# Three attention layers and a gate on one core: block sums in a scratch tile, a clip moved behind the exponential, biases added at the transposes

## The chip, the cores and the metric

The kernel runs on one core of a Trainium2 chip. The core has TensorE (matrix products into the eight banks of PSUM), VectorE, ScalarE and GpSimd for work on elements, and queues that start DMAs. The engines run side by side, each through its own instructions in order, and wait for each other at semaphores. The metric is the device time of one execution in microseconds (us), the median of several; the profile comes from one further execution with its own time.

## The reference

Sixteen samples of 256 channels by 32 x 32 positions (1024 tokens) pass through four layers. All numbers are float32.

```python
# layer 0: attention over tokens, on a group norm with 8 groups
xn = group_norm(x, gamma, beta)
q, k, v = split(einsum('bchw,oc->bohw', xn, w_qkv) + b_qkv)
out = softmax(q^T k / sqrt(256)) v ;  x = einsum(w_proj, out) + b_proj + x
# layer 1: a gate for each position
weight1, weight2 = mean(x, over channels), max(x, over channels)
weight3 = relu(conv3x3([weight1, weight2], w1, b1))
x = x * sigmoid(conv3x3(weight1 + weight2 + weight3, w2, b2))
# layer 2: as layer 0, with separate wq, wk, wv, wp and their biases
# layer 3: queries and keys of 32 channels, clipped logits
energy = clip(einsum('bqn,bqm->bnm', q, k) * 32**-0.5, -10, 10)
out = gamma * (v softmax(energy)^T) + x
```

In all three attentions the rows of the softmax add up to one, so a constant added to every value comes out of the attention as that same constant.

## The kernel before

**Folding.** At the start `fold` (L213) multiplies the weights of layers 0 and 2 together: `m` is the product of the query and key weights, `wvp` that of the value and output weights, and `brow` is the row of all value and output biases, on every partition. Layer 3 keeps its own weights `w3`, and `vg3` is its value bias times gamma.

**Two streams.** `sample(b)` (L683) is a generator that emits the work of one sample in small steps and yields after each. Two such streams, one over the even and one over the odd samples, are advanced in turn (L800 to L810); the first is ahead by `OFFSET` = 26 steps. A framework then assigns the semaphores and settles each engine's order, so that between two steps of one stream usually lies one of the other. While a sample is in layer 3, `head` (L672) loads sample b + 2, transposes it (`to_tokens`, L296) and normalizes it (`group_norm`, L87).

**PSUM.** All products use one pool of eight banks of 128 x 512 (`bank`, L183). A bank is used again when the last reader of its earlier content is done.

**One attention** (`attend`, L632; for layer 3 `clipped_attend`, L730) has these stages:

- `t = m x` in four products (L642) and, for the blocked products that follow, sums and differences `xs` of blocks of x (L656 to L659);
- the values (`values`, L326): four banks `vps`, each moved to `vt` with the bias added by VectorE (L663, or L752 in layer 3, which multiplies by gamma as well); then four combinations of value blocks (`tv`, L353 to L357). GpSimd writes columns of ones next to the values (L331, L351), so that the products also give the sums of the softmax;
- for each half of 512 queries, the logits. Layers 0 and 2 use seven block products in place of eight (`logits`, L387), whose sums are put together in the tile `e` by ScalarE copies (L435, L437, L444, L452) and VectorE additions (L432), and take the exponential on ScalarE (L448, L455). Layer 3 packs four 32-row products into four banks (L763), VectorE clips each bank into `e` (L772), and ScalarE takes the exponential of two at a time (L775);
- `weighted` (L458): the product of `e` with the values, again seven block products in place of eight. VectorE forms four combinations of `e` (L469, L470, L502, L505). Seven groups of eight products (each product is two instructions) go to three banks. Bank b holds the first product, then has `s2 t2` and later `s3 t3` added to it on TensorE, and is read in between; bank af holds two single products; bank c holds `s1 t1` and then has `s4` added. Each read is an `add` (L491): on VectorE, y = bank * ri + y, where `ri` is the reciprocal of the row sum (L510, L515) and y is the residual. A group that adds to a bank may start only when the reads of its earlier content are done.

After layer 0 comes the gate: VectorE takes sum and maximum over channels (L698), two small convolutions as products with banded matrices (`gate_of`, L124) give `sg`, VectorE multiplies the eight token blocks by it (L708), and TensorE transposes back to channels (`to_channels`, L317, with a ScalarE copy out of PSUM). `group_norm` computes statistics on VectorE (L93, L94), averages them over groups with two tiny products (`gm` L98, `gv` L107), a power on GpSimd (L111), and scales both blocks of channels on VectorE (L118). After layer 2 and layer 3 the tokens are transposed to channels in the same way; layer 3 sends them out by SyncE's queue (L781).

`count`, `alike` and `moderate` check that the sums and weights are in a safe range; otherwise a general path runs afterwards (`general_path`), which does not happen with these inputs.

Of the kernel before, what the change touches and what calls it, by code (L numbers as in the profile page):

```python
# [26 lines left out]
EPS = 1e-5  # L27

# [58 lines left out]
def group_norm(nc, k, small, psum, ptag, xt, out, gamma, beta, nm):  # L87
# [29 lines left out]
    for c in range(CC):  # L117
        nc.vector.tensor_scalar(  # L118
            out[:, c, :], xt[:, c, :], a[:, c : c + 1], bb[:, c : c + 1], ALU.mult, ALU.add
        )  # L120
# [40 lines left out]
def fast_path(nc, tc, k, bad, x, w_l0, w_l2, w_l3, qk_bias, v_bias, out):  # L161
# [7 lines left out]
    with ExitStack() as ctx:  # L169
# [30 lines left out]
        vcol = wts.tile([P, 2, CC], FP, name="vcol")  # L200
        for i in range(2):
            nc.sync.dma_start(vcol[:, i, :], v_bias[i].rearrange("(c p) -> p c", p=P))
        w3 = wts.tile([P, CC, 2 * DQK + C], FP, name="w3")
        nc.scalar.dma_start(w3, w_l3.rearrange("(c p) o -> p c o", p=P))
        vb3 = wts.tile([P, C], FP, name="vb3")
        nc.scalar.dma_start(vb3, v_bias[2:3, :].to_broadcast([P, C]))
# [6 lines left out]
        def fold(nm, which, base):  # L213
# [42 lines left out]
            nc.vector.tensor_scalar(tb, ps[:, :CC], C**-0.5, None, ALU.mult)  # L256

# [22 lines left out]
        vg3 = wts.tile([P, C], FP, name="vg3")  # L280
        gam = k.sc[:, S_GAMMA : S_GAMMA + 1]

        def fold3():
            for g in range(G4):
                i = g // 2
                nc.gpsimd.tensor_copy(
                    w3r[:, :, g * DQK : (g + 1) * DQK], w3[:, :, i * DQK : (i + 1) * DQK]
                )
            nc.vector.tensor_scalar(qb[:PH], qb[:PH], DQK**-0.5, None, ALU.mult)
            nc.vector.tensor_scalar(vg3, vb3, gam, None, ALU.mult)  # L290
# [5 lines left out]
        def to_tokens(xt, nm):  # L296

            xr = tokp.tile([P, NT, C], FP, tag="tok", name=f"xr_{nm}")
            for t2 in range(NT // 2):
# [17 lines left out]
        def to_channels(y, dst, h, c, nm):  # L317
# [6 lines left out]
            nc.scalar.copy(dst, ps)  # L324
# [133 lines left out]
        def weighted(e, vt, tv, y, ri, h, nm):  # L458
# [32 lines left out]
            def add(t, cs, ps):  # L491
                r = ri[:, t : t + 1]
                nc.vector.scalar_tensor_tensor(  # L493
                    y[:, t, cs], ps, r, y[:, t, cs], ALU.mult, ALU.add
                )
# [10 lines left out]
            go(a(1, 1), t4, af[:, 1])  # L506
            yield
# [41 lines left out]
        def alike(w, bias, nm):  # L549
# [14 lines left out]
            nc.vector.tensor_tensor(size[:, C:], bias, bias, ALU.mult)  # L564
            nc.vector.tensor_tensor(size[:, :C], ps[:, :C], size[:, C:], ALU.add)
# [59 lines left out]
        def checks():  # L625
# [4 lines left out]
            alike(w3[:, :, 2 * DQK :], vb3, "l3")  # L630

        def attend(xt, y, weights, nm):  # L632
# [27 lines left out]
            rows = brow.rearrange("p (o j c) -> p o j c", o=1, j=CC).to_broadcast([P, 2, CC, P])  # L660
# [22 lines left out]
        def sample(b):  # L683
# [6 lines left out]
            yield from attend(xt, xr, folded["l0"], f"l0_{b}")  # L690
# [15 lines left out]
            for h in range(NH):  # L706
                for t in range(h * TPH, (h + 1) * TPH):
                    nc.vector.tensor_scalar(  # L708
                        xr[:, t, :], xr[:, t, :], sg[:, t : t + 1], None, ALU.mult
                    )  # L710
                for c in range(CC):
                    to_channels(xr, x1[:, c, h * HALF : (h + 1) * HALF], h, c, f"x1_{b}")
# [17 lines left out]
        def clipped_attend(xt, y, b):  # L730

# [387 lines left out]
```

## Time and profile before

| | us |
|---|---|
| median of 3 runs | 3098.36 |
| all three | 3100.22, 3097.28, 3098.36 |
| the profiled execution | 3098.49 |
| its span, first to last instruction | 3096.6 |

The mean granted clock of TensorE was 0.986 of full speed. The kernel moves 19.56 MB in and 16.78 MB out, 12 GB/s over the span, so memory traffic is no subject here. The page gives, for each engine, the busy time; for groups of instructions (line, engine, operation, output <- input, shape) the busy time, the mean duration of one and the idle time of the engine just before them with what ended it. Groups that matter below (columns as described):

```profile
L493 DVE SCALAR_TENSOR_TENSOR xr_l<-b_l,ri_l,xr_l 128x128 f32<-128x128 f32 x256 | 77.9, 346 | 23.3 <-PE b_l L367 21.0
...
L532 DVE SCALAR_TENSOR_TENSOR xr_l<-b_l,ri_l,xr_l 128x256 f32<-128x256 f32 x128 | 56.1, 480 | 65.4 <-PE b_l L367 65.1
```

In these rows DVE is VectorE, ACT ScalarE, POOL GpSimd, PE TensorE and PEld its loading of weights. A matmul instruction of the list is half of one float32 product, so the counts are twice those of the code. A wait for several semaphores is put down to the one that came last.

### The profile page before, as it was taken

What the parts mean: (1) busy time and instruction counts of PE and PEld (TensorE: products, weight loads), DVE (VectorE), ACT (ScalarE), POOL (GpSimd) and SP (SyncE); (2) the same over time, 40 slices, a digit from 0 to 9 for tenths busy, and PEclk for the clock granted to TensorE, in tenths of its full rate; (3) what the DMA queues carried; (4) which work ended last, traced back from release to release, by engine and by line L of the source; (5) the groups of instructions that cost most, each with busy time, mean ns of one, the idle gap of its engine ahead of it and who ended that gap; (6) DMA issues with size and microseconds to landing.
All of it is one profiled execution on the core that took longest, in us unless ns stands there. A gap on an engine that the chain in (4) does not pass through costs nothing.

```text
span 3096.6 us, 44611 instructions
## 1 busy us (share of the span) xinstructions
PE 2937.3 (95%) x18586; PEld 2528.2 (82%) x18586; DVE 2203.7 (71%) x4587; ACT 933.6 (30%) x1329; POOL 55.6 (2%) x231
## 2 busy tenths in 40 slices
PE   7999999999999999999999999999999999999997
PEld 6878878878888788788887887888878888788886
DVE  8677776777766767677676777677776677767675
ACT  1223233233233332333232322323333323223232
POOL 0000000000000000000000000000000000000000
PEclk9999999999999999999999999999999999999999
DMA  1000000000000000000000000000000000000000
GB/s 64 1 1 14 21 14 8 1 14 28 8 8 1 14 28 8 8 1 14 28 15 1 15 1 28 15 1 14 1 28 15 1 15 20 9 15 1 1 8 22
DMA packets 16159, 39.25 MB, mean 13 GB/s; under 512 B 2640, under 2 KB 3152, under 8 KB 15952
## 3 DMA queue, kind: packets, MB, share of 16 engines
q1 hardware_dynamic: 14560, 33.56, 3.1%
q8 instruction: 148, 2.42, 0.3%
q10 hardware_dynamic: 1392, 2.78, 0.2%
q14 instruction: 59, 0.48, 0.1%
HBM read 19.56 MB, written 16.78 MB: 12 GB/s over the span
## 4 chain that ended last, share of the span: by engine, by line
PE 79%; DVE 18%; ACT 1%; issue 1%; POOL 1%; DMA 1%; ACTq 0%; DVEq 0%
PE b_l L367 13%; PE vps_l L337 10%; PE sb_l L367 10%; PE c_l L367 10%; PE tp_l L642 7%; PE sc_l L367 7%; PE af_l L367 6%; PE sa_l L367 4%; PE sf_l L367 4%; DVE e L772 3%; PE qk L739 2%; DVE cb_l L469 2%; PE s L763 2%; DVE xr_l L493 2%; PE yp_x L321 1%; DVE e_l L432 1%
## 5 line engine op out<-in xcount | busy, mean ns | idle before, releaser
L367 PEld LDWEIGHTS b_l<-vt_l,e_l 128*128 128x128 f32 x2048 | 245.3, 192 | 21.1 <-DVE xr_l L493 7.9
L367 PE MATMUL b_l<-vt_l,e_l 128*128 128x128 f32 x2048 | 255.9, 276 | 6.1 <-DVE xr_l L493 5.6
L337 PE MATMUL vps_l<-wvp_l,x 128*128 128x256 f32 x1024 | 242.7, 380 | 0.0
L642 PE MATMUL tp_l<-x,m_l 128*128 128x512 f32 x512 | 230.2, 592 | 0.0
L435 ACT COPY e_l<-sb_l 128x512 f32<-128x512 f32 x128 | 75.2, 588 | 464.0 <-PE sb_l L367 464.0
L775 ACT ACTIVATE e<-e 128x1024 f32<-128x1024 f32 x128 | 134.3, 1055 | 258.1 <-DVE e L772 251.1
L337 PEld LDWEIGHTS vps_l<-wvp_l,x 128*128 128x128 f32 x1024 | 189.9, 190 | 23.7 <-DVE tap L82 0.2
L444 ACT COPY e_l<-sb_l 128x512 f32<-128x512 f32 x128 | 75.0, 586 | 426.0 <-PE sb_l L367 424.9
L367 PE MATMUL c_l<-tv_l,cb_l 128*128 128x129 f32 x1536 | 192.9, 277 | 0.0
L367 PEld LDWEIGHTS c_l<-tv_l,cb_l 128*128 128x128 f32 x1536 | 183.8, 192 | 6.7 <-issue 5.3
L367 PE MATMUL c_l<-vt_l,e_l 128*128 128x129 f32 x1024 | 135.7, 288 | 43.1 <-DVE xr_l L493 42.2
L448 ACT ACTIVATE e_l<-e_l 128x1024 f32<-128x1024 f32 x128 | 135.4, 1057 | 129.0 <-DVE e_l L432 128.1
L642 PEld LDWEIGHTS tp_l<-x,m_l 128*128 128x128 f32 x512 | 94.1, 190 | 94.8 <-issue 84.6
L367 PEld LDWEIGHTS c_l<-vt_l,e_l 128*128 128x128 f32 x1024 | 126.9, 200 | 53.7 <-issue 43.5
L432 DVE TENSOR_TENSOR e_l<-sc_l,e_l 128x512 f32<-128x512 f32 x128 | 88.3, 690 | 111.0 <-PE sc_l L367 111.0
L650 ACT ACTIVATE t_l<-tp_l,tb_l 128x512 f32<-128x512 f32 x128 | 88.0, 687 | 251.5 <-PE tp_l L642 251.2
L772 DVE TENSOR_SCALAR e<-s 128x512 f32<-128x512 f32 x256 | 159.6, 685 | 5.6 <-PE s L763 5.6
L455 ACT ACTIVATE e_l<-e_l 128x1024 f32<-128x1024 f32 x128 | 135.1, 1061 | 55.6 <-DVE e_l L432 54.1
L367 PE MATMUL sa_l<-t_l,x 128*128 128x256 f32 x512 | 139.7, 397 | 0.0
L367 PEld LDWEIGHTS b_l<-vt_l,e 128*128 128x128 f32 x1024 | 123.8, 194 | 16.9 <-ACT e L775 8.0
L367 PE MATMUL sf_l<-tc_l,x 128*128 128x256 f32 x512 | 137.6, 393 | 0.0
L367 PE MATMUL sb_l<-tc_l,xs_l 128*128 128x256 f32 x512 | 134.2, 382 | 1.3 <-ACT e_l L435 1.3
(190 smaller groups left out, 5931.4 us busy)
## 6 DMA issues: line engine op xcount, KB each, us to landing
x<-in_x_dram SPq DMA_DIRECT2D x32, 512.0 KB, 4.4
out_dram<-oc SPq DMA_DIRECT2D x64, 256.0 KB, 2.2
raw_l<-in_w_l_dram ACTq DMA_DIRECT2D x2, 1024.0 KB, 7.8
w<-in_w_l_dram ACTq DMA_DIRECT2D x1, 320.0 KB, 4.0
tidx<-in_tap_idx_dram ACTq DMA_DIRECT2D x1, 192.0 KB, 6.6
vb<-in_v_bias_dram ACTq DMA_DIRECT2D x1, 128.0 KB, 6.4
qb<-in_qk_bias_dram SPq DMA_DIRECT2D x4, 0.1 KB, 5.8
vcol<-in_v_bias_dram SPq DMA_DIRECT2D x2, 1.0 KB, 7.3
```

What stands on the lines that cost most here:

```text
L337: nc.tensor.matmul(ps[:, i * C : (i + 1) * C], src[:, c, t * P : (t + 1) * P], w[:, c, col : col + C], start=(c == 0), stop=(c == CC - 1),)
L367: mm = nc.tensor.matmul(out, left, right, start=fresh and m == 0 and (lone or i == 0), stop=(m == len(pairs) - 1), skip_group_check=True,)
L432: nc.vector.tensor_tensor(dst, two(ps), dst, ALU.add)
L435: nc.scalar.copy(block(0, 0), two(b))
L444: nc.scalar.copy(block(0, 1), two(b))
L448: nc.scalar.activation(e[:, m : m + 2, :], e[:, m : m + 2, :], AF.Exp)
L455: nc.scalar.activation(e[:, m : m + 2, :], e[:, m : m + 2, :], AF.Exp)
L469: nc.vector.tensor_tensor(s1, a(1, 0), a(1, 1), ALU.add)
L642: nc.tensor.matmul(ps, m[:, c, o * P : (o + 1) * P], xt[:, c, hs], start=(c == 0), stop=(c == CC - 1),)
L650: nc.scalar.activation(tt[:, o, hs], ps, AF.Identity, bias=tb[:, o : o + 1], scale=C**-0.5)
L772: nc.vector.tensor_scalar(e[:, mm, :], ss[g], -10.0, 10.0, ALU.max, ALU.min)
L775: nc.scalar.activation(part, part, AF.Exp)
```

## The change

The change has these parts:

- **Block sums.** `weighted` gets a scratch tile `acc`. ScalarE copies the first content of each block (`acc[lo, c1]`, `acc[hi, c2]`, `acc[lo, c2]`, `acc[hi, c1]`), VectorE adds the others to it (`plus`, 256 elements each), and when a token block is complete, `done` computes y = acc * ri + y once for 256 channels. `s2 t2` is now emitted ahead of `s4`.
- **Layer 3 clip.** ScalarE takes the exponential straight from the PSUM bank, and GpSimd clips two at a time to exp(-10) and exp(10).
- **Value biases.** Layers 2 and 3 no longer add the bias to the values; ScalarE copies these out (layer 3 with gamma as scale). The bias of layer 2 is added at the transposes of its result (`bcol2`), and that of layer 3 at the output's transposes, together with `bcol2` (the tokens y do not hold it) as `bcol3`. A third bias column is loaded in place of the row `vb3`.
- **Gate.** A function `planes`, called after each half of layer 0, takes the maximum on VectorE and the mean on ScalarE (a copy with an accumulated sum, one for each token block). ScalarE multiplies every other token block by the gate.
- **Norm and tokens.** `group_norm` scales its second block of channels on ScalarE; `to_tokens` copies all four banks by ScalarE and yields twice in place of three times.

```diff
+EXP_MIN, EXP_MAX = math.exp(-10.0), math.exp(10.0)
...
-    for c in range(CC):
-        nc.vector.tensor_scalar(
-            out[:, c, :], xt[:, c, :], a[:, c : c + 1], bb[:, c : c + 1], ALU.mult, ALU.add
-        )
+    nc.vector.tensor_scalar(out[:, 0, :], xt[:, 0, :], a[:, 0:1], bb[:, 0:1], ALU.mult, ALU.add)
+    nc.scalar.activation(
+        out[:, 1, :], xt[:, 1, :], AF.Identity, bias=bb[:, 1:2], scale=a[:, 1:2]
+    )
...
-        vcol = wts.tile([P, 2, CC], FP, name="vcol")
-        for i in range(2):
+        vcol = wts.tile([P, 3, CC], FP, name="vcol")
+        for i in range(3):
             nc.sync.dma_start(vcol[:, i, :], v_bias[i].rearrange("(c p) -> p c", p=P))
         w3 = wts.tile([P, CC, 2 * DQK + C], FP, name="w3")
         nc.scalar.dma_start(w3, w_l3.rearrange("(c p) o -> p c o", p=P))
-        vb3 = wts.tile([P, C], FP, name="vb3")
-        nc.scalar.dma_start(vb3, v_bias[2:3, :].to_broadcast([P, C]))
+
+        bcol2 = wts.tile([P, CC], FP, name="bcol2")
+        bcol3 = wts.tile([P, CC], FP, name="bcol3")
...
+            if nm == "l2":
+
+                ps = bank(f"brp_{nm}")
+                for c in range(CC):
+                    for o in range(CC):
+                        nc.tensor.matmul(
+                            ps[:, c : c + 1],
+                            wp[:, o, c * P : (c + 1) * P],
+                            vcol[:, which, o : o + 1],
+                            start=(o == 0),
+                            stop=(o == CC - 1),
+                        )
+                nc.vector.tensor_tensor(bcol2, ps[:, :CC], k.vec[:, :, base + 4], ALU.add)
+                return m, wvp, tb, None
...
-            nc.vector.tensor_scalar(vg3, vb3, gam, None, ALU.mult)
+            nc.vector.scalar_tensor_tensor(
+                bcol3, vcol[:, 2, :], gam, bcol2, ALU.mult, ALU.add
+            )
...
+                nc.scalar.copy(dst, ps)
                 if t2 % 2:
-                    nc.vector.tensor_copy(dst, ps)
-                else:
-                    nc.scalar.copy(dst, ps)
                     yield xr
-            yield xr
...
-            nc.scalar.copy(dst, ps)
+            if bias is None:
+                nc.scalar.copy(dst, ps)
+            else:
+                nc.scalar.activation(dst, ps, AF.Identity, bias=bias[:, c : c + 1])
...
-            def add(t, cs, ps):
-                r = ri[:, t : t + 1]
+            c1, c2 = slice(0, P), slice(P, C)
+            lo, hi = slice(0, 2), slice(2, 4)
+            acc = combp.tile([P, TPH, C], FP, tag="acc", name=f"acc_{nm}_{h}")
+
+            def plus(ts, cs, ps):
+                nc.vector.tensor_tensor(acc[:, ts, cs], ps, acc[:, ts, cs], ALU.add)
+
+            def done(i):
+                t = h * TPH + i
                 nc.vector.scalar_tensor_tensor(
-                    y[:, t, cs], ps, r, y[:, t, cs], ALU.mult, ALU.add
-                )
-
-            c1, c2 = slice(0, P), slice(P, C)
+                    y[:, t, :], acc[:, i, :], ri[:, t : t + 1], y[:, t, :], ALU.mult, ALU.add
+                )
+
             b = bank(f"b_{nm}_{h}")[:, : 2 * P].rearrange("p (i c) -> p i c", i=2)
             go(a(0, 0), vb(0, 0), b, lone=False)
+            nc.scalar.copy(acc[:, lo, c1], b)
             yield
             af = bank(f"af_{nm}_{h}").rearrange("p (w i c) -> p w i c", w=2, i=2)
             nc.vector.tensor_tensor(s2, s1, s2, ALU.subtract)
...
             yield
             nc.vector.tensor_tensor(s4, s4, s2, ALU.subtract)
             go(a(1, 1), t4, af[:, 1])
+            plus(lo, c1, af[:, 0])
             yield
             c = bank(f"c_{nm}_{h}")[:, : 2 * (P + 1)].rearrange("p (i c) -> p i c", i=2)
             go(s1, t1, c, lone=False)
             nc.vector.reciprocal(ri[:, n1 : n1 + 2], c[:, :, P])
-            for i in range(2):
-                add(n1 + i, c2, c[:, i, :P])
+            nc.scalar.copy(acc[:, hi, c2], c[:, :, :P])
+            yield
+            go(s2, t2, b, fresh=False)
+            nc.scalar.copy(acc[:, lo, c2], b)
             yield
             go(s4, vb(1, 1, P + 1), c, fresh=False)
             nc.vector.reciprocal(ri[:, n0 : n0 + 2], c[:, :, P])
+            plus(lo, c2, c[:, :, :P])
             for i in range(2):
-                add(n0 + i, c1, b[:, i, :])
-            for i in range(2):
-                add(n0 + i, c2, c[:, i, :P])
-            for i in range(2):
-                add(n0 + i, c1, af[:, 0, i, :])
-            yield
-            go(s2, t2, b, fresh=False)
-            for i in range(2):
-                add(n0 + i, c2, b[:, i, :])
+                done(i)
             yield
             go(s3, t3, b, fresh=False)
-            for i in range(2):
-                add(n1 + i, c1, af[:, 1, i, :])
-            for i in range(2):
-                t = n1 + i
-                nc.vector.scalar_tensor_tensor(
-                    y[:, t, :].rearrange("p (j c) -> p j c", j=CC),
-                    b[:, i : i + 1, :].to_broadcast([P, CC, P]),
-                    ri[:, t : t + 1],
-                    y[:, t, :].rearrange("p (j c) -> p j c", j=CC),
-                    ALU.mult,
-                    ALU.add,
-                )
+            nc.scalar.copy(acc[:, hi, c1], b)
+            plus(hi, c2, b)
+            plus(hi, c1, af[:, 1])
+            for i in range(2, 4):
+                done(i)
             yield
 
...
-                    nc.vector.tensor_tensor(dst, ps, rows, ALU.add)
+                    if brow is None:
+                        nc.scalar.copy(dst, ps)
+                    else:
+                        nc.vector.tensor_tensor(dst, ps, rows, ALU.add)
...
+                if then is not None:
+                    then(h)
...
+            def planes(h):
+                ts = slice(h * TPH, (h + 1) * TPH)
+                nc.vector.tensor_reduce(
+                    pl[:, 1, 1 + h * TPH : 1 + (h + 1) * TPH], xr[:, ts, :], AX.X, ALU.max
+                )
+                for t in range(h * TPH, (h + 1) * TPH):
+                    junk = work.tile([P, HALF], FP, tag="oc", name=f"junk_{b}_{t}", bufs=3)
+                    nc.scalar.activation(
+                        junk[:, :C],
+                        xr[:, t, :],
+                        AF.Copy,
+                        scale=1.0 / C,
+                        accum_out=pl[:, 0, 1 + t : 2 + t],
+                    )
+
+            yield from attend(xt, xr, folded["l0"], f"l0_{b}", planes)
             if b == 0:
                 k.build_toep(nc, work)
             elif b == 1:
                 checks()
-            for h in range(NH):
-                ts = slice(h * TPH, (h + 1) * TPH)
-                for i, op in enumerate((ALU.add, ALU.max)):
-                    nc.vector.tensor_reduce(
-                        pl[:, i, 1 + h * TPH : 1 + (h + 1) * TPH], xr[:, ts, :], AX.X, op
-                    )
-            nc.vector.tensor_scalar(pl[:, 0, :], pl[:, 0, :], 1.0 / C, None, ALU.mult)
...
-                    nc.vector.tensor_scalar(
-                        xr[:, t, :], xr[:, t, :], sg[:, t : t + 1], None, ALU.mult
-                    )
-                for c in range(CC):
-                    to_channels(xr, x1[:, c, h * HALF : (h + 1) * HALF], h, c, f"x1_{b}")
+                    if t % 2:
+                        nc.scalar.activation(
+                            xr[:, t, :], xr[:, t, :], AF.Copy, scale=sg[:, t : t + 1]
+                        )
+                    else:
+                        nc.vector.tensor_scalar(
+                            xr[:, t, :], xr[:, t, :], sg[:, t : t + 1], None, ALU.mult
+                        )
+                for c in range(CC):
+                    to_channels(xr, x1[:, c, h * HALF : (h + 1) * HALF], h, c, None, f"x1_{b}")
...
-                for c in range(CC):
-                    to_channels(xr, x2[:, c, h * HALF : (h + 1) * HALF], h, c, f"x2_{b}")
+                hs = slice(h * HALF, (h + 1) * HALF)
+                for c in range(CC):
+                    to_channels(xr, x2[:, c, hs], h, c, bcol2, f"x2_{b}")
...
-                    nc.vector.scalar_tensor_tensor(dst, ps, gam, rows, ALU.mult, ALU.add)
+                    nc.scalar.activation(dst, ps, AF.Copy, scale=gam)
...
-                        nc.vector.tensor_scalar(e[:, mm, :], ss[g], -10.0, 10.0, ALU.max, ALU.min)
+                        nc.scalar.activation(e[:, mm, :], ss[g], AF.Exp)
                         if g % 2:
                             part = e[:, mm - 1 : mm + 1, :]
-                            nc.scalar.activation(part, part, AF.Exp)
+                            nc.gpsimd.tensor_scalar(
+                                part, part, EXP_MIN, EXP_MAX, ALU.max, ALU.min
+                            )
...
-                    to_channels(y, oc, h, c, f"o_{b}")
+                    to_channels(y, oc, h, c, bcol3, f"o_{b}")
```

More of the change, by code (lines that the diff above doesn't have):

```diff
@@ L1 @@
+import math
 from contextlib import ExitStack
@@ L279, in fast_path @@
         w3r = wts.tile([P, CC, P], FP, name="w3r")
-        vg3 = wts.tile([P, C], FP, name="vg3")
         gam = k.sc[:, S_GAMMA : S_GAMMA + 1]
@@ L309, in to_tokens, with to_channels @@
                 dst = xr[:, 2 * t2 : 2 * t2 + 2, :].rearrange("p t c -> p (t c)")
+                nc.scalar.copy(dst, ps)
                 if t2 % 2:
-                    nc.vector.tensor_copy(dst, ps)
-                else:
-                    nc.scalar.copy(dst, ps)
                     yield xr
-            yield xr
-        def to_channels(y, dst, h, c, nm):
+        def to_channels(y, dst, h, c, bias, nm):
             ps = bank(f"yp_{nm}_{h}_{c}")
@@ L563, in alike @@
             size = work.tile([P, HALF], FP, tag="oc", name=f"sz_{nm}", bufs=3)
-            nc.vector.tensor_tensor(size[:, C:], bias, bias, ALU.mult)
-            nc.vector.tensor_tensor(size[:, :C], ps[:, :C], size[:, C:], ALU.add)
+            if bias is None:
+                nc.vector.tensor_copy(size[:, :C], ps[:, :C])
+            else:
+                nc.vector.tensor_tensor(size[:, C:], bias, bias, ALU.mult)
+                nc.vector.tensor_tensor(size[:, :C], ps[:, :C], size[:, C:], ALU.add)
             ends = small.tile([P, 2], FP, tag="ends", name=f"ends_{nm}")
@@ L629, in checks, with attend @@
                 moderate(m, tb, base, nm)
-            alike(w3[:, :, 2 * DQK :], vb3, "l3")
-        def attend(xt, y, weights, nm):
+            alike(w3[:, :, 2 * DQK :], None, "l3")
+        def attend(xt, y, weights, nm, then=None):
             m, wvp, tb, brow = weights
@@ L659, in attend @@
             nc.vector.tensor_tensor(xs[:, 3], xt[:, 1, lo], xs[:, 1], ALU.subtract)
-            rows = brow.rearrange("p (o j c) -> p o j c", o=1, j=CC).to_broadcast([P, 2, CC, P])
+            if brow is not None:
+                rows = brow.rearrange("p (o j c) -> p o j c", o=1, j=CC)
+                rows = rows.to_broadcast([P, 2, CC, P])
             for vt, dst, ps, tv in values(xt, wvp, 0, nm):
                 if tv is None:
-                    nc.vector.tensor_tensor(dst, ps, rows, ALU.add)
+                    if brow is None:
+                        nc.scalar.copy(dst, ps)
+                    else:
+                        nc.vector.tensor_tensor(dst, ps, rows, ALU.add)
                 yield
@@ L689, in sample @@
             nc.gpsimd.memset(gp, 0.0)
-            yield from attend(xt, xr, folded["l0"], f"l0_{b}")
+            def planes(h):
[13 more added lines that the diff above has]
+            yield from attend(xt, xr, folded["l0"], f"l0_{b}", planes)
             if b == 0:
@@ L707, in sample @@
                 for t in range(h * TPH, (h + 1) * TPH):
-                    nc.vector.tensor_scalar(
-                        xr[:, t, :], xr[:, t, :], sg[:, t : t + 1], None, ALU.mult
-                    )
+                    if t % 2:
+                        nc.scalar.activation(
+                            xr[:, t, :], xr[:, t, :], AF.Copy, scale=sg[:, t : t + 1]
+                        )
+                    else:
+                        nc.vector.tensor_scalar(
+                            xr[:, t, :], xr[:, t, :], sg[:, t : t + 1], None, ALU.mult
+                        )
                 for c in range(CC):
-                    to_channels(xr, x1[:, c, h * HALF : (h + 1) * HALF], h, c, f"x1_{b}")
+                    to_channels(xr, x1[:, c, h * HALF : (h + 1) * HALF], h, c, None, f"x1_{b}")
                 yield
@@ L748, in clipped_attend @@
                 yield
-            rows = vg3.rearrange("p (o j c) -> p o j c", o=1, j=CC).to_broadcast([P, 2, CC, P])
             for vt, dst, ps, tv in values(xt, w3, 2 * DQK, f"l3_{b}"):
                 if tv is None:
-                    nc.vector.scalar_tensor_tensor(dst, ps, gam, rows, ALU.mult, ALU.add)
+                    nc.scalar.activation(dst, ps, AF.Copy, scale=gam)
                 yield
```

## The prediction

> **What bounds the kernel now.** I read the page's busy shares first, then the groups by shape, then what TensorE waited for, then the time line of one period.
>
> ```profile
> PE 2937.3 (95%) x18586; PEld 2528.2 (82%) x18586; DVE 2203.7 (71%) x4587; ACT 933.6 (30%) x1329; POOL 55.6 (2%) x231
> ...
> PE 79%; DVE 18%; ACT 1%; issue 1%; POOL 1%; DMA 1%; ACTq 0%; DVEq 0%
> ```
>
> The chain that ended last is TensorE for 79% and VectorE for 18%; ScalarE and GpSimd hardly appear in it and are mostly idle. So TensorE's own work is the floor, and VectorE is what keeps TensorE off it. The first question is how far off.
>
> ```profile
> 767.00:1146.00 379.00, 363.42 (x2310) 313.09 (x2310) 270.12 (x556) 116.64 (x167) 6.65 (x26) 0.99 0.04 12
> ```
>
> The stretches table (columns: stretch, length, busy of PE, PEld, DVE, ACT, POOL, granted clock) repeats itself: two samples take 378.9 us, eight times. In undisturbed stretches the time line gives 1.785 us for 16 products of 128 columns (111.6 ns each), 1.73 us for 8 of 256 (216 ns), 3.44 us for 8 of 512 (430 ns), 1.07 us for 8 of the packed 32-row form (134 ns) and 0.876 us for 8 transposes (109.5 ns). Per period there are 1344, 640, 80, 64 and 128 of these: 150.0 + 138.4 + 34.4 + 8.6 + 14.0, plus some 5 for the small ones = 350.5 us. So 378.9 - 350.5 = 28.4 us of each period (227 us over eight) is waiting; 15.6 of the 28.4 stand as idle, the rest lies inside groups drawn longer than their cadence. What ends the idle part:
>
> ```profile
> PE c_l L367 <- DVE xr_l L493: 44.1, 33, 2.8
> PE gv_l L107 <- DVE d_l L104: 21.1, 10, 10.0
> PE gm_l L98 <- DVE mv_l L94: 18.5, 9, 2.2
> PE s L763 <- DVE e L772: 14.8, 7, 2.1
> PE yp_x L321 <- DVE xr_l L708: 12.6, 8, 1.6
> PE b_l L367 <- DVE xr_l L493: 10.2, 18, 0.9
> PE af_l L367 <- ACT e L775: 9.2, 9, 1.1
> ```
>
> (Columns: total us, times, longest.) Nearly all are VectorE, late by its queue: `c_l` waits because the second group into bank c may only start when the reciprocal and two adds have read the first, and they stand behind other work. The time line of the worst case:
>
> ```profile
> 1073.08 0.16 DVE L510 RECIPROCAL ri_l<-c_l 128x2 f32<-128x2 f32 x1
> ...
> 1073.88 1.53 DVE L118 TENSOR_SCALAR x<-x,a_l,bb_l 128x1024 f32<-128x1024 f32 x2
> 1075.32 0.60 DVE L493 SCALAR_TENSOR_TENSOR xr_l<-c_l,ri_l,xr_l 128x128 f32<-128x128 f32 x2
> 1075.84 2.48 DVE L772 TENSOR_SCALAR e<-s 128x512 f32<-128x512 f32 x4
> 1076.07 3.04 PE L367 MATMUL c_l<-vt_l,e_l 128*128 128x129 f32 x16 [2.76 <-DVE xr_l L493]
> 1077.22 2.19 ACT L775 ACTIVATE e<-e 128x1024 f32<-128x1024 f32 x2 [16.37 <-DVE e L772]
> ```
>
> The reader sees the other stream's norm and clip queue around the adds, TensorE waiting 2.76 us, and ScalarE free for 16.37 us.
>
> **The change, engine by engine.** VectorE loses: the clip L772, 159.6 us; L752, 47.9; L663 for layer 2, half of 88.1 = 44; the sum half of L698 and L701, 41; half of L118, 24.5; half of L708, 18; L311, 22. The block adds were 77.9 + 77.4 + 77.3 + 39.0 + 38.6 + 37.0 + 56.1 + 28.0 = 431 us; they become, 96 times, 4 `plus` of 256 elements (0.42 us, as L400's row) and 4 `done` (0.48, as L532's) = 347. In all 357 + 84 = 441 less: 1763 us, 58%.
>
> ScalarE gains, with copies at 588 ns per 512 (L435), so some 375 per 256: 384 first sums, 144 us; layer 2 and 3 values, 64 x 0.59 + 64 x 0.69 = 82; exponentials straight from PSUM, 256 x 0.66 (between L435 and L650) less 134.3 = 35; half norms, 32 x 1.1 (L448) = 35; 32 token copies 19, 64 gate products 28, 128 channel sums at about 0.45 = 58, bias on 128 transposes 13. Together 414: 1348 us, 44%. Neither is a bound by its sum.
>
> GpSimd gains 128 clips of 128x1024, an operation the trace does not have. Its memsets (204 ns for 128 elements, 104 for 4) give 0.8 ns per element and 0.95 us, the lower end; its copy of 64 in 235 ns, over a memset's 100 ns of start, gives 2.1 and 2.26 us, the upper; the affine select, 128 in 292 ns, is the nearest (one input from SBUF, computed): 1.5 ns and 1.6 us, which I take. The Trainium skill (GPSIMD Engine Reference, Engine selection) calls one-input operations roughly line-rate; at its 1.2 GHz that would be an estimate of 0.85 us plus a start, and the sum below would lose its 12 us of clip cost.
>
> What changes on the path, over the run:
>
> 1. `c_l` and `b_l` behind L493, 54.3 us idle. The first sums are copied by ScalarE, and `s2 t2` now lies between the two groups into bank c, while `s4` lies between the last two into bank b: a full group of 1.79 us and a step of the other stream more. The reciprocals stay on VectorE and still read bank c first. I take 45 gained.
> 2. Stretch of those groups: `c_l<-vt_l,e_l` is busy 135.7 us where 1024 x 111.6 ns is 114. Half, 10.
> 3. Layer 3 logits: 14.8 idle, and the 512 products are busy 108.2 where 134 ns each makes 68.6, 39.6 more. Eight evictions take ScalarE 8 x 0.66 = 5.3 us against VectorE's 4.9, but ScalarE's queue is empty there, where L772 started at 796.68 for products done from 791.9. In its place come the other stream's copies and exponentials, 4.5 us per four steps. Half of 54.4, 27.
> 4. `yp_x` behind L708: half of the products go to ScalarE, 6 of 12.6.
> 5. `gm` and `gv`: their short chain stays on VectorE, with less queued before it: 8 of 39.6.
> 6. `planes` writes into the three buffers that the output tiles use, so a ScalarE copy could wait for an output's landing (2.2 us, at most 32 x 2.2 = 70). In the period the outputs start near 828, 863, 1110 and 1144 us, and the halves of layer 0 end near 850, 901, 936 and 985: 13 us apart or more, so 0.
> 7. Start: the layer 2 bias row and one 128 KB load go, small transfers and products come; under 1 us beside work that bounds, taken as 0.
>
> Gains 96. Costs: after the last exponential the old order had nothing more to do, now two clips. From the first logits product, the fourth clip ends at 1.4 + 4 x 1.6 = 7.8 us against 4.9 + 1.06 = 6.0 before; TensorE comes to the first product that reads it (`af`) after 1.07 + 1.73 + 1.07 + 1.73 + 1.79 + 1.73 = 9.1 us. So the other stream's steps hide it while a clip stays under (9.1 - 1.4) / 4 = 1.9 us; without that cover, as in the last sample, each half is 1.8 us late. Behind the clips stand `rstd` and the ones columns on GpSimd, and behind `s1 = a + b` on VectorE, which waits for the last clip, the other stream's adds. I charge 12 for this, and 4 for ScalarE copies met late. At the end of each half, copy, two adds and two `done` take about 1.9 us where 0.88 stood; a step of the other stream (1.7 us or more) covers it, and without it 96 x 1.0 us would be lost at most.
>
> Net 96 - 16 = 80. The profiled run took 3098.49 (span 3096.6 and 1.9 around it), 0.1 over the median of 3098.36: **3018 us**.
>
> A sign against the clip shows already: `rstd`, 694 ns as a median, took 1.13 when VectorE read two SBUF tensors.
>
> ```profile
> 790.14 0.69 DVE L354 TENSOR_TENSOR tv_l<-vt_l,tv_l 128x512 f32<-128x512 f32 x1
> 790.25 1.13 POOL L111 TENSOR_TENSOR rstd_l<-ve_l,neg_half 128x2 f32<-128x2 f32 x1 [26.86 <-DVE ve_l L109]
> ...
> 923.24 0.69 POOL L111 TENSOR_TENSOR rstd_l<-ve_l,neg_half 128x2 f32<-128x2 f32 x1 [14.56 <-DVE ve_l L109]
> ```
>
> VectorE's operations with two SBUF inputs (block combinations 470, tv 132, xs 87, tc 108, and now `done`, which had PSUM before, 184) fill about a third of the time; a clip would lose a third of 0.5 us, 0.17, and end under the 1.9 still. The Trainium skill (SBUF — State Buffer, SBUF: two separate sides) says more: the pair of ports is an exclusive lock, and whoever comes second waits for the whole instruction. By it VectorE too would lose up to a third of 128 x 1.6 us, some 70 us, out of 1330 that it has idle; on the path that could eat most of the 80.
>
> **Rivals.** *ScalarE holds instead (0.17).* In the logits of layer 3 its 5.3 us plus the other stream's 2 to 3 us meet 5.6 us of TensorE. Of this, 1.5 us late in each of 32 halves costs 48 in place of the 4: 3098.5 - 96 + 12 + 48 = 3062. For it: all 384 copies and 256 exponentials are in one queue. Against it: only 30% busy now, and idle 16 us before such a phase.
>
> *GpSimd holds, slower (0.15).* From an effective 1.9 us per clip, waits for VectorE included, each further 0.1 costs 0.4 us in 32 halves, 12.8 us; the 80 are gone at 2.5 us. At 3.0: 3018 + 11 x 12.8 = 3159. For it: the upper bound of 2.26 us plus contention. Against it: two of three rows.
>
> *Nothing to tell (0.08).* The waits move on: `gm`, `gv` and the banks hold TensorE as long as before, 3097. For it: eight banks for two streams remain. Against it: ten times more idle ends at L493 and L772 than at any bank freed by ScalarE.
>
> That the kernel loses clock by running denser is unlikely: 0.99 was granted over the period, 1.00 in the stretch of 50 to 100 us, where TensorE was busy for 48.86 of 50.
>
> **Numbers.** Forecast 0.60, own range 2965 to 3070. Low end: all 124.6 us of idle that VectorE ends and half of the logits' stretch (20) go, 2954. High end: 2.6 us per clip, 3018 + 7 x 12.8 = 3108. A measurement tells 0.2%, 6 us, from no change; faster takes the forecast and most of the first rival, 0.76, same 0.07, slower 0.17.
>
> **What would show it.** Right: VectorE near 1760 us, ScalarE near 1350, a 378.9 us period near 369, no `c_l` wait behind VectorE, clips under 1.9 us. Wrong: `af` or `cb` waiting for clips over 60 us in sum, clips over 2.5 us, or logits still waiting for banks.

## The result, and the profile after

The changed kernel takes 3192.70 us (median of 4 runs, 3190.01 to 3195.59) against 3098.86 us: ratio 1.0303, 95% interval 1.0285 to 1.0321. It is 3.0% slower. The forecast was 3018 us, the range 2954 to 3108.

The page after, in the parts that answer to those shown of before (busy time of each engine; shares of the chain that ended last, by engine and by line):

```profile
span 3193.8 us, 44752 instructions
...
PE 2960.3 (93%) x18582; PEld 2560.7 (80%) x18582; DVE 1781.2 (56%) x3445; ACT 1278.4 (40%) x2353; POOL 523.6 (16%) x359
...
PE 74%; POOL 15%; DVE 5%; ACT 4%; issue 1%; DMA 0%; ACTq 0%; SPq 0%; DVEq 0%
```

VectorE fell from 2203.7 to 1781.2 us, near the 1763 of the forecast, and its share of the chain from 18% to 5%. GpSimd, 1% of the chain before, now has 15%. What TensorE waited for (total us, times, longest):

```profile
PE b_l L385 <- POOL e L814: 112.4, 56, 4.3
PE af_l L385 <- POOL e L814: 58.3, 40, 2.9
PE gv_l L109 <- DVE d_l L106: 19.2, 17, 6.9
```

The waits behind VectorE's adds, clips and norm statistics (L493, L772, L94 of before) are gone, all but `gv`; in their place stand 170.7 us behind the GpSimd clip. The clip's group, by shape (busy us, mean ns | idle before it), and its spread (minimum, median, maximum ns):

```profile
L814 POOL TENSOR_SCALAR e<-e 128x1024 f32<-128x1024 f32 x128 | 474.1, 3727 | 536.4 <-ACT e L811 536.4
L814 POOL TENSOR_SCALAR e<-e x128: 3613/3618/4605, 324.0 to 3167.1; 128x1024 f32<-128x1024 f32 x128
```

One clip takes 3.62 us, more than twice the 1.6 us of the forecast and above its upper end of 2.26. One half of layer 3, in order of time (start, length):

```profile
425.01 1.14 PE L802 MATMUL s<-qk 32*128 32x512 f32 x8
...
426.51 2.07 ACT L811 ACTIVATE e<-s 128x512 f32<-128x512 f32 x4 [2.43 <-PE s L802]
...
427.68 14.45 POOL L814 TENSOR_SCALAR e<-e 128x1024 f32<-128x1024 f32 x4 [6.89 <-ACT e L811]
427.80 1.53 DVE L375 TENSOR_TENSOR vt_l<-vt_l 128x512 f32<-128x512 f32 x1
...
429.25 0.68 DVE L373 TENSOR_TENSOR tv_l<-vt_l,tv_l 128x512 f32<-128x512 f32 x1
...
429.85 0.68 DVE L676 TENSOR_TENSOR xs_l<-x,xs_l 128x512 f32<-128x512 f32 x1
...
431.43 0.71 PE L385 MATMUL b_l<-vt_l,e 128*128 128x128 f32 x4 [0.35 <-POOL e L814]
435.01 2.93 PE L385 MATMUL b_l<-vt_l,e 128*128 128x128 f32 x12 [2.87 <-POOL e L814]
...
442.17 1.23 DVE L487 TENSOR_TENSOR cb_l<-e 128x1024 f32<-128x1024 f32 x1 [11.03 <-POOL e L814]
442.19 1.61 PE L385 MATMUL af_l<-vt_l,e 128*128 128x128 f32 x12 [1.94 <-POOL e L814]
```

Four clips run one behind the other for 14.45 us. The group into bank b starts behind the first, stands after four instructions until the second has ended, and `af` stands until the fourth. From the first logits product (425.01) to the first product on the last clip's data (442.19) pass 17.2 us; VectorE waits for 11 us in the same place, because `cb` needs that clip too.

### The profile page after: what moved, and what is told of

Read it like the earlier page. It is cut to its first block, busy times and chain, and to the rows that moved or that the text cites. A ratio compares the mean times of both kernels' runs of the same rounds, so it can differ in the third digit from the quotient of the medians.

```text
span 3193.8 us, 44752 instructions
## 1 busy us (share of the span) xinstructions
PE 2960.3 (93%) x18582; PEld 2560.7 (80%) x18582; DVE 1781.2 (56%) x3445; ACT 1278.4 (40%) x2353; POOL 523.6 (16%) x359
## 4 chain that ended last, share of the span: by engine, by line
PE 74%; POOL 15%; DVE 5%; ACT 4%; issue 1%; DMA 0%; ACTq 0%; SPq 0%; DVEq 0%
POOL e L814 15%; PE b_l L385 12%; PE c_l L385 10%; PE vps_l L355 9%; PE sb_l L385 9%; PE af_l L385 8%; PE tp_l L659 7%; PE sc_l L385 6%; PE sa_l L385 3%; PE sf_l L385 3%; PE yp_x L336 1%; PE qk L779 1%; ACT e L811 1%; PE yp_o L336 1%; PE s L802 1%
## 5 line engine op out<-in xcount | busy, mean ns | idle before, releaser
L814 POOL TENSOR_SCALAR e<-e 128x1024 f32<-128x1024 f32 x128 | 474.1, 3727 | 536.4 <-ACT e L811 536.4
L385 PE MATMUL b_l<-vt_l,e 128*128 128x128 f32 x1024 | 163.2, 317 | 112.4 <-POOL e L814 112.4
L487 DVE TENSOR_TENSOR cb_l<-e 128x1024 f32<-128x1024 f32 x32 | 39.2, 1226 | 384.5 <-POOL e L814 384.5
L385 PEld LDWEIGHTS b_l<-vt_l,e 128*128 128x128 f32 x1024 | 147.4, 224 | 127.2 <-POOL e L814 125.9
L462 ACT COPY e_l<-sb_l 128x512 f32<-128x512 f32 x128 | 75.1, 587 | 276.0 <-PE sb_l L385 275.8
L537 ACT COPY acc_l<-c_l 128x256 f32<-128x256 f32 x96 | 35.7, 372 | 366.4 <-DVE ri_l L536 329.5
L450 DVE TENSOR_TENSOR e_l<-sa_l,e_l 128x512 f32<-128x512 f32 x128 | 87.9, 687 | 127.9 <-PE sa_l L385 120.3
L811 ACT ACTIVATE e<-s 128x512 f32<-128x512 f32 x256 | 133.8, 617 | 47.4 <-PE s L802 47.4
```

What stands on the lines that cost most here:

```text
L385: mm = nc.tensor.matmul(out, left, right, start=fresh and m == 0 and (lone or i == 0), stop=(m == len(pairs) - 1), skip_group_check=True,)
L450: nc.vector.tensor_tensor(dst, two(ps), dst, ALU.add)
L462: nc.scalar.copy(block(0, 1), two(b))
L487: nc.vector.tensor_tensor(s1, a(1, 0), a(1, 1), ALU.add)
L537: nc.scalar.copy(acc[:, hi, c2], c[:, :, :P])
L811: nc.scalar.activation(e[:, mm, :], ss[g], AF.Exp)
```

## The experiments

Two theories. *Theory 1*: the length of the GpSimd clip is the whole loss, and the rest of the change is a gain. *Theory 2*: the rest costs too, in ScalarE's queue or in the new sums. Times are medians; each ratio is to the kernel before, timed beside it on the same chip.

| run | us | ratio and 95% interval |
|---|---|---|
| clip on VectorE, on exponentials | 2936.95 | 0.9479 (0.9466 to 0.9491) |
| clip on VectorE, on logits | 2976.28 | 0.9608 (0.9593 to 0.9622) |
| GpSimd clip alone, in the kernel before | 3299.68 | 1.0650 (1.0633 to 1.0666) |
| no clip | 2935.28 | 0.9473 (0.9459 to 0.9488) |
| GpSimd clip of one operation | 3072.49 | 0.9919 (0.9902 to 0.9935) |
| one bank in four on GpSimd | 2938.45 | 0.9487 (0.9471 to 0.9503) |
| clip on VectorE, old sums | 3019.32 | 0.9742 (0.9726 to 0.9758) |
| clip on VectorE, old gate, norm, token copies | 2943.06 | 0.9502 (0.9486 to 0.9518) |
| clip on VectorE, values by VectorE | 2936.09 | 0.9474 (0.9458 to 0.9489) |
| block sums alone | 3010.75 | 0.9715 (0.9698 to 0.9731) |
| GpSimd clip, first group reordered | 3223.91 | 1.0399 (1.0382 to 1.0417) |
| the same with the wait filled | 3239.51 | 1.0451 (1.0433 to 1.0468) |

**Where the clip stands.** The first run moves one word:

```diff
-                            nc.gpsimd.tensor_scalar(
+                            nc.vector.tensor_scalar(
                                 part, part, EXP_MIN, EXP_MAX, ALU.max, ALU.min
                             )
```

> The changed kernel with the clip of the exponentials on VectorE instead of GpSimd (128 x 128x1024, SBUF to SBUF, near the 0.81 us of L119). Theory 1, the length of the GpSimd clip (3.62 us as a median, 14.4 us for the four of a half) is the whole loss: the 171 us that TensorE waits for it and some 30 us of stretched groups go, VectorE grows from 1781 to about 1885 us: 2970 to 3020 us. Theory 2, the rest of the change costs too (ScalarE's queue late with first sums, the sums themselves longer): over 3060 us.

Measured 2936.95 us: 256 below the changed kernel and 161 below the kernel before. Theory 1 holds, and even its gain was set too small: the time lies below its interval. The clip's row on VectorE, and the place shown above, in this kernel:

```profile
L814 DVE TENSOR_SCALAR e<-e 128x1024 f32<-128x1024 f32 x128 | 85.8, 690 | 34.7 <-ACT e L811 34.2
```

```profile
410.59 1.14 PE L802 MATMUL s<-qk 32*128 32x512 f32 x8
...
415.76 1.89 DVE L814 TENSOR_SCALAR e<-e 128x1024 f32<-128x1024 f32 x3
...
416.49 1.95 PE L385 MATMUL b_l<-vt_l,e 128*128 128x128 f32 x16
...
420.00 1.95 PE L385 MATMUL af_l<-vt_l,e 128*128 128x128 f32 x16
```

690 ns each, and TensorE goes from the logits to `af` in 9.41 us without a wait, where the GpSimd clips made it 17.18. Counted to the end of the `af` group, the means over all 32 halves of the two traces are 11.27 and 19.03 us: 7.76 us more, 248 over the 32 halves, against 256 measured.

The second run puts the old clip of the logits and the exponential after it back (the two lines of L772 and L775 of the kernel before).

> The changed kernel with the old clip of the logits on VectorE (256 x 0.685 us out of PSUM) and the old exponential after it. Theory 1: as with the clip of the exponentials on VectorE, but some 60 us more on VectorE and its queue before the banks again: 3000 to 3050 us. Theory 2: over 3080 us.

2976.28 us, in the interval: the clip on the exponentials, with ScalarE reading the banks, is worth 39 us by itself when VectorE does it. VectorE is busy 1927.6 us with the old order and 1857.7 with the new.

The third puts the exponential from PSUM and the GpSimd clip into the kernel before and changes nothing else.

> The kernel before with only the layer 3 exponential from PSUM and the GpSimd clip. Theory 1: the clip's loss alone, without the gains of the rest: 3240 to 3310 us, clips of 3.6 us, TensorE waiting 150 us or more for them. Theory 2: the clip is a small part, 3100 to 3190 us.

3299.68 us: alone the part costs 202 us. TensorE's waits in it:

```profile
PE b_l L369 <- POOL e L777: 88.2, 33, 4.3
PE c_l L369 <- DVE xr_l L495: 54.3, 33, 3.5
PE af_l L369 <- POOL e L777: 50.9, 34, 2.9
```

139 us behind the clip, somewhat under the 150 expected, beside the old waits for the adds, which are all still there. The time is in the expected interval.

The fourth leaves the clip out.

> The changed kernel without the layer 3 clip (left out). The floor for every place of the clip. Theory 1: 2960 to 3000 us, at most 30 below the clip on VectorE. Theory 2: over 3050 us.

2935.28 us, 1.7 below the clip on VectorE: there the clip costs next to nothing, and there is no better place to look for. (Theory 1 expected 2960 us at the least.)

**What a GpSimd clip costs.** Two runs measure the price. In the first the clip is one operation, the minimum; the lower bound is left out.

```diff
-                            nc.gpsimd.tensor_scalar(
-                                part, part, EXP_MIN, EXP_MAX, ALU.max, ALU.min
-                            )
+                            nc.gpsimd.tensor_scalar(part, part, EXP_MAX, None, ALU.min)
```

> The changed kernel with a GpSimd clip of one operation (the minimum; the lower bound is left out). If GpSimd pays per operation and element, an instruction falls from 3.62 to some 1.9 us, which the step between hides: TensorE waits under 40 us for it and the time is 2940 to 2990 us. If it pays per element whatever the operations, 3.6 us and 3190 us as before.

Neither: the clip takes 2.76 us and the kernel 3072.49. In the second, the first bank of each group of four is clipped by GpSimd, one bank at a time, the other three by VectorE:

```diff
-                        if g % 2:
-                            part = e[:, mm - 1 : mm + 1, :]
-                            nc.gpsimd.tensor_scalar(
-                                part, part, EXP_MIN, EXP_MAX, ALU.max, ALU.min
-                            )
+                        part = e[:, mm, :]
+                        eng = nc.gpsimd if g == 0 else nc.vector
+                        eng.tensor_scalar(part, part, EXP_MIN, EXP_MAX, ALU.max, ALU.min)
```

> The changed kernel with the clip of one bank in four on GpSimd (128x512, the first of each group of four) and of the other three on VectorE. If the cost is linear in elements, the GpSimd instruction takes 1.8 to 1.9 us, ends before the last VectorE clip, and the time is that of the clip on VectorE, 2930 to 2950 us. If GpSimd's share of the ports or a fixed cost decides, over 2970 us.

2938.45 us, as expected, though the instruction was longer than expected (2.2 us in the mean). The GpSimd rows of the two kernels, in this order (minimum, median, maximum ns):

```profile
L814 POOL TENSOR_SCALAR e<-e x128: 2757/2763/3575, 324.1 to 3048.4; 128x1024 f32<-128x1024 f32 x128
```

```profile
L814 POOL TENSOR_SCALAR e<-e x64: 1913/2024/3023, 322.6 to 2913.4; 128x512 f32<-128x512 f32 x64
```

An estimate from the minima 1913 (512 elements) and 3613 ns (1024): two operations cost (3613 - 1913) / 512 = 3.32 ns per element and 213 ns besides. One operation less saves (3613 - 2757) / 1024 = 0.84 ns per element. If the first operation costs as much as the second, 1.65 are left for an element without any; no run has such a clip. The time follows the length: with 2.76 us per clip the four, and the 2.67 us from the first product to the first clip (425.01 to 427.68 above), make 13.71 us, 4.30 over the 9.41 without a wait, times 32 = 138 us; measured 3072.49 - 2936.95 = 136.

**Which parts gained.** Three runs undo one part each of the best kernel (clip on VectorE). The first takes the old `weighted` with its `add`:

```diff
-            nc.scalar.copy(acc[:, lo, c1], b)
...
+            for i in range(2):
+                add(n1 + i, c2, c[:, i, :P])
```

> The clip on VectorE with the block sums as before (adds from each bank into y, s2 t2 after s4). If these waits were the main gain, the 54 us of TensorE behind the adds come back with their drop in clock: 2995 to 3030 us. If the gain is VectorE's load as a whole, a part in proportion to 77 us of 346 less: 2960 to 2980 us.

3019.32 us, 82 more: the waits by name. VectorE is busy 103 us more (1960.7), and 52.4 us of TensorE's idle time before groups into banks b and c end at VectorE again, 45.0 of them at the adds:

```profile
PE c_l L385 <- DVE xr_l L511: 35.5, 33, 1.5
...
PE b_l L385 <- DVE xr_l L511: 9.5, 16, 0.9
PE c_l L385 <- DVE gp L144: 7.4, 8, 0.9
```

The second puts the channel sums, the gate products, the second half of the norm and the token copies back on VectorE (the lines removed by the change at these four places).

> The clip on VectorE with the channel sums, the gate products, the second half of the norm and the token copies back on VectorE as before (some 106 us more there). If only waits by name count, some 30 us come back (norm statistics 18.5, gate 12.6): 2960 to 2975 us. If the load counts in proportion, 106 of 346: 2980 to 3000 us.

2943.06 us, 6 more: under both expectations, and the two intervals overlap. In the profiled execution (2937.22 us, no slower than the best kernel) the `yp_x` wait comes back (10.2 us for 3.5), the norm's do not; with the sums and the clip moved, VectorE has room for this work.

The third lets VectorE take the values of layers 2 and 3 out of PSUM; the biases stay at the transposes.

```diff
-                        nc.scalar.copy(dst, ps)
+                        nc.vector.tensor_copy(dst, ps)
...
-                    nc.scalar.activation(dst, ps, AF.Copy, scale=gam)
+                    nc.vector.tensor_scalar(dst, ps, gam, None, ALU.mult)
```

> The clip on VectorE, with the values of layers 2 and 3 taken out of PSUM by VectorE again (128 x 0.69 us, 88 us there; the biases stay at the transposes). If VectorE's load counts only where banks and sums wait, within 10 us of 2937; if it counts in proportion (162 us for 346), some 40 us: 2975 to 2985 us.

2936.09 us, no difference, with VectorE busy 1936.9 us and not 1857.7: its load by itself counts for nothing here.

A fourth run keeps only the block sums, with all the other work back on VectorE. The biases must stay at the transposes: the rows that they replace leave no room for the scratch tile.

> Of the change only the block sums, and the biases at the transposes that make room for their scratch tile; clip, values, channel sums, gate, norm and token copies on VectorE as before. If the gains add up, 82 us as in the run that undid the sums: 3005 to 3030 us. If VectorE's load has to fall elsewhere too before they count, 3050 us or more.

3010.75 us, 89 below the kernel before that was timed beside it (3099.70): the sums bring their gain without the rest.

**The clock after a wait.** Between the changed kernel and the best one TensorE's idle time differs by 171 us (233.5 and 62.9, spans less busy times) and its busy time by 88 (2960.3 and 2872.5). The second part is products that run slowly. The stretches of the changed kernel (the granted clock is the number after POOL's):

```profile
716.00:720.00 4.00, 1.12 (x10) 0.91 (x9) 0.00 (x0) 0.94 (x3) 4.00 (x3) 1.00 0.00 0
720.00:722.00 2.00, 2.00 (x14) 1.91 (x15) 0.00 (x0) 0.37 (x1) 2.00 (x1) 0.85 0.03 8
722.00:725.00 3.00, 3.00 (x10) 2.37 (x9) 0.00 (x0) 0.59 (x2) 3.00 (x2) 0.53 0.00 0
```

After a wait of 2.88 us (717.1 to 720.0) the clock falls to 0.53. To see what this costs, a pair of runs reorders the first group (the four products of the first clip pair, then those of the second) and, in the second of them, puts ten products between, which write columns that nobody reads:

```diff
+                product([(b[:, 0, :], one[:2]), (b[:, 1, :], two[:2])], True, False)
+                for _ in range(FILL):
+                    nc.tensor.matmul(
+                        fill, left[:, 1, :P], right[:, 1, :],
+                        start=False, stop=True, skip_group_check=True,
+                    )
+                product([(b[:, 0, :], one[2:]), (b[:, 1, :], two[2:])], False, True)
```

With FILL = 0:

> Control for the next run: the changed kernel (GpSimd clip) with the first layer 3 group of each half in another order, the four products of the first clip pair ahead of the four of the second. The clip still ends when it ends, so both theories: 3175 to 3200 us.

With FILL = 10:

> As the control, with 10 more products (20 instructions of 112 ns, 2.2 us) per half in the place where TensorE waits for the second clip pair; they write columns that nobody reads. If the stretched groups after the waits (88 us more busy than with the clip on VectorE) are a lowered TensorE clock after idle time, work that keeps TensorE busy there makes the kernel faster by 35 to 75 us: 3115 to 3160 us, granted clock over 0.985. If the groups are stretched by late data, the filling gains nothing: 3180 to 3230 us.

The control took 3223.91 us, 31 more than the changed kernel, and the filled kernel 3239.51, 16 more again: both are misses, above every interval that was given for them. The same half without and with the filling:

```profile
1106.88 1.14 PE L817 MATMUL s<-qk 32*128 32x512 f32 x8
...
1116.47 1.59 PE L386 MATMUL b_l<-vt_l,e 128*128 128x128 f32 x8 [2.43 <-POOL e L829]
1117.86 1.91 PE L386 MATMUL sb_l<-t_l,x 128*128 128x256 f32 x4
...
1123.65 2.76 PE L386 MATMUL af_l<-vt_l,e 128*128 128x128 f32 x12 [2.17 <-POOL e L829]
```

```profile
1109.60 1.14 PE L817 MATMUL s<-qk 32*128 32x512 f32 x8
...
1116.60 2.40 PE L532 MATMUL b_l<-vt_l,e 128*128 128x128 f32 x20
1119.19 1.16 PE L386 MATMUL b_l<-vt_l,e 128*128 128x128 f32 x8 [0.19 <-POOL e L829]
1120.19 1.03 PE L386 MATMUL sb_l<-t_l,x 128*128 128x256 f32 x4
...
1126.37 2.93 PE L386 MATMUL af_l<-vt_l,e 128*128 128x128 f32 x12 [2.88 <-POOL e L829]
```

Behind the first wait the filling does what it should to the clock: four instructions of `sb` take 1.03 us and not 1.91. But from the logits to `af` it is 16.77 us in both. What the products save, the wait for the fourth clip takes: the clips run one after the other and end when they end. So the lowered clock after the first wait costs nothing there; what is slow after the last wait of a half can cost. The group that follows this wait, in the changed kernel, the control and the filled kernel (busy us, mean ns | idle before it):

```profile
L385 PE MATMUL af_l<-vt_l,e 128*128 128x128 f32 x512 | 76.0, 294 | 58.3 <-POOL e L814 58.3
```

```profile
L386 PE MATMUL af_l<-vt_l,e 128*128 128x128 f32 x512 | 95.3, 346 | 79.8 <-POOL e L829 79.8
```

```profile
L386 PE MATMUL af_l<-vt_l,e 128*128 128x128 f32 x512 | 106.8, 376 | 114.9 <-POOL e L829 114.9
```

In the best kernel it is busy 62.7 us. So 19 of the control's 31 us and 12 of the further 16 lie in this one group: in both runs slow products come to stand behind the last wait, where nothing hides them. In the half shown its twelve instructions take 2.76 and 2.93 us, at a granted clock of 0.55 and 0.51, where the half of the changed kernel shown further up has 1.61. The rest of the two differences was not assigned.

## Why the prediction was wrong, point by point

**The step that failed is the price of a clip.** "1.5 ns and 1.6 us, which I take", with 0.95 and 2.26 us as ends. The runs show 3.62 us: by the estimate above 213 ns and 3.32 ns per element, 0.84 of it for the second operation. The rows drawn on were a memset (no input), a copy of 64 columns (no arithmetic) and a select; none held two operations, and each was extrapolated over 8 to 16 times its length. The second operation alone, 0.86 us per clip, was in no row. The true price lay outside both ends. Two of the forecast's own signs of being wrong came with it: clips over 2.5 us, and `cb` waiting for clips, 384.5 us in sum.

**The point from which it decides was set somewhat too late.** A clip may last 1.9 us, said the forecast, from 9.1 us of cover less 1.4 until the first clip starts. The cover was right: the best kernel shows 9.41 us. The start was not: in the half shown the first exponential starts 1.50 us after the first logits product and the first clip 2.67 us after it. That leaves (9.41 - 2.67) / 4 = 1.69 us. This alone would have changed little, since the 1.6 us taken still fit. Each 0.1 us beyond was priced at 12.8 us; between clips of 2.76 and 3.62 us the runs show 3192.70 - 3072.49 = 120 for 0.86, 14.0 for 0.1. So the rival "GpSimd holds, slower", with a chance of 0.15 and 3159 us at 3.0 us, was the right mechanism: by its own rule 3.62 us costs 17.2 x 12.8 = 220 us, from 1.69 us on it would be 247, and 256 were measured. Its weight was too small because the clip's range was too narrow.

**The gains were right in kind and too small:** 161 us in place of 96.

- Sums (points 1 and 2, 55 us): 82 undone alone, 89 done alone.
- Layer 3 logits (point 3, 27): 39, by the clip on logits against that on exponentials.
- Gate and norm (points 4 and 5, 14): 6 at the end, with intervals that overlap, when VectorE is no longer late.
- The values, counted as load only: 0.
- What is left, 161 - 82 - 39 - 6 = 34 us, was not split further: it may be gains that any of two parts brings, or those of pieces not undone by themselves.

Over the run, idle time fell by 96 (159.3 to 62.9) and busy time by 65 (2937.3 to 2872.5). The forecast saw the stretched groups and took them half for waits that stay. In the kernel before, the clock rows show what they are:

```profile
797.00:800.00 3.00, 2.58 (x4) 0.99 (x4) 3.00 (x6) 1.86 (x2) 0.00 (x0) 0.50 0.00 0
800.00:803.00 3.00, 3.00 (x8) 2.44 (x8) 2.35 (x5) 2.37 (x3) 0.00 (x0) 0.50 0.00 0
```

These six microseconds follow the 2.11 us wait for L772, at half the clock. A mean of 0.99 over the period, which the forecast read, hides them. The mean is 0.986 before, 0.995 in the best kernel and 0.972 in the changed one.

**ScalarE** was forecast at 1348 us and is busy 1278.4; it holds nothing, and its rival fell: no wait of TensorE over 1 us ends at ScalarE.

**GpSimd and VectorE's shared ports.** The rule of the Trainium skill (SBUF — State Buffer, SBUF: two separate sides) is that whoever comes second waits for the whole instruction. For GpSimd the trace agrees: the longest clip, 4.61 us, started 0.1 us after an L527 of VectorE (1.23 us, two SBUF inputs). For VectorE it does not: L375, two SBUF inputs, started 0.12 us after a clip and took 1.53 us (0.685 as a median), less than the 3.6 us of the clip, and L373 and L676, two SBUF inputs each, took 0.68 in the midst of the clips, as elsewhere. In sum it is little: the clips lose 474.1 - 128 x 3.618 = 11 us, L375 grows by 5.8. The "most of the 80" that the forecast set beside it did not come. The other page that was cited (GPSIMD Engine Reference, Engine selection), with one-input operations at roughly line-rate, does not fit: an estimate of 0.85 us and a start by it, 3.62 us measured.

## What to carry to other kernels

Before work moves to an engine that has no row of that operation, measure one instruction of the real size and with the real number of operations; bounds that come from shorter and simpler instructions are no bounds. An engine at 16% can still set the time: what counts is how long its chain of dependent instructions is against the other work that lies between producer and consumer, here 4 x 3.62 us against the 6.7 us (9.41 - 2.67) that lie in between. A change of many parts is worth taking apart: with the one clip on VectorE it is 5.2% faster than the kernel before and not 3.0% slower.

## What the hardware showed that was not expected

GpSimd's two-operation clip of 128x1024 float32 takes 3.61 us where VectorE does it, SBUF to SBUF with constants, in 0.69: 5.2 times as long; the second of the two operations costs GpSimd 0.84 ns per element. VectorE takes 0.81 us for the same shape where it multiplies and adds by columns (L119); which of the two, the operations or the columns, makes the difference was not tried. A short wait of TensorE can halve its clock: in the kernel before, one of 2.11 us was followed by 6 us at 0.50, and in the changed kernel one of 2.88 us by 2 us at 0.85 and 3 us at 0.53. It need not: after 2.24 us behind `gm` (918.4 to 920.6 us, before) and after two waits of 2.87 us (from 1208.2 and 1215.3 us, changed kernel) the clock stayed at 1.00, so the length of the wait alone does not decide, and what else does was not found. The Trainium skill (TensorE: Matmul & The Clock Gate, Part 1: The HAM clock gate) gives an idle window of about 3.4 us for the drop; the 2.11 us wait in the kernel before already sufficed. Products that nobody needs kept the clock up behind the first wait, but the drop came behind the last one, and the kernel was 16 us slower.
